# W2's Hadamard transform in pieces within attention's steps, the running sum ahead of the transposes, and tile-wise reuse of memory

## The chip, the cores and the metric

The kernel runs on one core of one Trainium2 chip. The metric is the device time of one execution in microseconds; three runs of the kernel before gave a median of 3984.01 us (3983.97 to 3985.0). Engines are named TensorE (PE in the profile), VectorE (DVE), ScalarE (ACT), GpSimd (POOL) and SyncE (SP), whose queue issues every transfer of this kernel.

## The reference, cut to what matters

One transformer layer with post-norms on x of 2 x 2048 x 512, all in f32:

```python
q, k, v, s = heads(x @ Wq), heads(x @ Wk), heads(x @ Wv), clip(heads(x @ Ws), -32, 32)
z = cumlogsumexp(s, axis=time)            # 16 heads, 64 keys, 64 slots, 128 values
p, g = exp(s - z), exp(shift(z) - z)
hk = scan(hk * g + k p);  pv = softmax(q hk)   # over the 64 slots
hv = scan(hv * g + p v);  o = pv hv
o = rmsnorm(o) * g_norm_weight * silu(x @ Wg)
x = layernorm(x + o @ Wo)
hidden = silu(x @ W1.T) * (x @ W3.T)      # 2048 wide
hidden = fwht(hidden)                     # Walsh-Hadamard transform, scaled by 1/sqrt(2048)
x = layernorm(x + hidden @ W2.T)
```

The transform is linear and symmetric, so it can be applied to W2 (512 x 2048) once instead of to `hidden` for every token. The kernel does that, before and after the change.

## The kernel before, in words

**Products.** Every large matrix product is a 2 x 2 block product made with 7 block multiplications instead of 8 (Strassen's scheme). `LEFT` and `RIGHT` (L89, L90) say which sums of blocks enter product k, `SUM` (L91) into which of the three PSUM sums c1, c2, c3 it is accumulated. For that, weights and activations are kept as 7 blocks: three as they are, and four sums and differences.

**W2's transform (L104 to L152).** In front of everything else. For each of four 128-row tiles of W2, it loads four pieces of 128 x 512 (L120), transposes each on TensorE (L125), multiplies them by a 128 x 128 Hadamard matrix (L130), which does 7 of the 11 butterfly stages, and does the other 4 on VectorE (L139, L140), each as an addition and a subtraction of 1024 columns. Then the 7 blocks are formed for each of 8 column blocks (L146 to L151), and stored to `w2s` in DRAM in one transfer of 896 KB each (L152).

**Attention (L161 to L654).** 4 groups of 4 heads, and in each 16 steps of 128 time positions for both batches: 64 steps. `run` (L551) writes a step's work by hand, in one order for TensorE, VectorE, ScalarE and GpSimd (`manual_schedule`): the products of this step (`now`), the second half of attention of the step before (`before`), the output projection that ends the one before that (`old`), and the input of the next (`new`). SP's queue is not in that order: a scheduler places the transfers. In the parts that the change touches:

- q1 to q7 are the products with `wqks` (L320), v1 to v7 those with `wvg` (L350), o1 to o7 those with `wo` (L533). `into` (L267) copies products 1, 5 and 6 on ScalarE (L273) and adds the others to them on VectorE (L278). o's results are added to `rows` (L529), which `store_rows` writes to `yd` (L546). Each engine works through its queue in order.
- `ps` is one PSUM tile of four banks, used in turn by `make_x` (L302), r's transposes (L452), the scores (L397, L400, L459, L464), `slots` (L412, L419), `values` (L476, L482), k's and E's transposes (L371, L373), the running sum (L378) and o's transposes (L517).
- `values` ends with a square on ScalarE (L487), a product on VectorE (L489), the addition to hv (L494) and a sum (L496). The next use of `ps` by TensorE is `k_e_transposed` (L367), copied out by L375; after one product of v, `running_sum` (L377) multiplies `e2` by a triangular matrix, z is copied (L380), and its reciprocal is taken in two halves (L389). The `scores` (L397) follow after another product of v, and their masking (L405), which `slots` (L412) needs.
- The first `Weights` are loaded ahead of the steps, `wqks`, `wvg` and `wo` in this order, and their four sums each (`sums`, L211) are made there, before any step. In later groups loads and sums lie within the steps. All weights share one buffer for the fourth block (`low`).

**FFN (L657 to L840).** Two halves of 16 tiles of 128 tokens. `load_tokens` reads `yd` (L676), transposes and forms 7 blocks, `load_weights` does so for W1 and W3 in the first half, `up` makes the two products and the gate, `down` the product with W2's blocks from `w2s` (L786, L799). Its pools are opened when attention's are closed. A pool's first tiles then wait until all of what lay in that memory is done.

The lines are those of the profile:

Of the kernel before, what the change touches and what calls it, by code (L numbers as in the profile page):

```python
# [14 lines left out]
P = 128  # L15
# [18 lines left out]
def gated_slot_attention_ffn_kernel(  # L34
# [69 lines left out]
    with ExitStack() as prep:  # L104
        rawp = prep.enter_context(tc.tile_pool(name="rawp", bufs=4))
        hp = prep.enter_context(tc.tile_pool(name="hp", bufs=2))
        wp = prep.enter_context(tc.tile_pool(name="w2p", bufs=1))
        ptp = prep.enter_context(tc.tile_pool(name="ptp2", bufs=4, space=PSUM))
        ppj = prep.enter_context(tc.tile_pool(name="ppj2", bufs=4, space=PSUM))
        hm = rawp.tile([P, P], F32, name="hm", bufs=1)  # L110
        nc.sync.dma_start(out=hm, in_=had)
        w2h = wp.tile([P, NFB, D], F32, name="w2h")

        for dt in range(KC):
            t0 = hp.tile([P, NFB, P], F32, name="t0")
            for q in range(NFB // 4):
                raw = rawp.tile([P, 4 * P], F32, name="raw")
                nc.sync.dma_start(  # L120
                    out=raw, in_=w2[dt * P : (dt + 1) * P, q * 4 * P : (q + 1) * 4 * P]
                )
                tp = ptp.tile([P, 4, P], F32, name="tp")
                for c in range(4):
                    nc.tensor.transpose(tp[:, c, :], raw[:, c * P : (c + 1) * P], ident)  # L125
                nc.scalar.copy(t0[:, 4 * q : 4 * q + 4, :], tp)
            t1 = hp.tile([P, NFB, P], F32, name="t1")
            for q in range(NFB // 4):
                pj = ppj.tile([P, 4, P], F32, name="pj")
                nc.tensor.matmul(pj, lhsT=hm, rhs=t0[:, 4 * q : 4 * q + 4, :], start=True, stop=True)  # L130
                nc.scalar.copy(t1[:, 4 * q : 4 * q + 4, :], pj)
            src, dst = t1, t0
            s = 1
            while s < NFB:
                if 2 * s == NFB:
                    dst = w2h[:, :, dt * P : (dt + 1) * P]
                a = src.rearrange("p (a two s) d -> p a two s d", two=2, s=s)
                o = dst.rearrange("p (a two s) d -> p a two s d", two=2, s=s)
                nc.vector.tensor_tensor(o[:, :, 0], a[:, :, 0], a[:, :, 1], ALU.add)  # L139
                nc.vector.tensor_tensor(o[:, :, 1], a[:, :, 0], a[:, :, 1], ALU.subtract)  # L140
                src, dst = dst, src
                s *= 2
        for hb in range(NPB):
            b = [w2h[:, hb + i * NPB, j * HD : (j + 1) * HD] for i in range(2) for j in range(2)]
            wt = hp.tile([P, 7, HD], F32, name="wt")
            nc.scalar.copy(wt[:, 0, :], b[0])  # L146
            nc.scalar.copy(wt[:, 1:3, :], w2h[:, hb + NPB, :].rearrange("p (j d) -> p j d", j=2))
            nc.vector.tensor_tensor(wt[:, 3, :], b[1], b[0], ALU.subtract)
            nc.gpsimd.tensor_tensor(wt[:, 5, :], b[3], b[1], ALU.subtract)
            nc.vector.tensor_tensor(wt[:, 4, :], b[3], wt[:, 3, :], ALU.subtract)  # L150
            nc.vector.tensor_tensor(wt[:, 6, :], b[2], wt[:, 4, :], ALU.subtract)  # L151
            nc.sync.dma_start(out=w2s[hb], in_=wt)  # L152

# [7 lines left out]
    with ExitStack() as att:  # L161
        wp = att.enter_context(tc.tile_pool(name="wp", bufs=1))
        xp = att.enter_context(tc.tile_pool(name="xp", bufs=2))
        yp = att.enter_context(tc.tile_pool(name="yp", bufs=6))
        keep = att.enter_context(tc.tile_pool(name="keep", bufs=1))
        c2 = att.enter_context(tc.tile_pool(name="c2", bufs=2))
        c1 = att.enter_context(tc.tile_pool(name="c1", bufs=1))
        pps = att.enter_context(tc.tile_pool(name="pps", bufs=1, space=PSUM))
# [5 lines left out]
        def bank(at, width=P):  # L174
            return ps[:, at].rearrange("p (i t) -> p i t", t=width)
# [371 lines left out]

        steps = [Step(g, n) for g in range(NG) for n in range(NCB)]
        w, nw = {}, {}

        def run(new, now, before, old):  # L551
# [10 lines left out]
            opens = now is not None and now.first  # L562

# [4 lines left out]
            do(new, "load_x")  # L568
# [4 lines left out]
            if opens and g:  # L573
                nw["vg"].sums(0)
# [5 lines left out]
            if opens and g:  # L580
                nw["vg"].sums(1)
            do(now, "q", 6)
            if opens and g:
                nw["vg"].sums(2)
            do(now, "q", 3)
            do(old, "store_rows")
# [3 lines left out]
            if opens and g:  # L590
                nw["vg"].sums(3)
# [10 lines left out]
            if o_last:  # L602
                nw["o"].sums(0)
            do(now, "k_e_transposed")
            do(now, "v", 2)
            if o_last:
                nw["o"].sums(1)
            do(now, "running_sum")
# [6 lines left out]
            if o_last:  # L615
                nw["o"].sums(2)
# [12 lines left out]
            if o_last:  # L629
                nw["o"].sums(3)  # L630
# [11 lines left out]
        with tc.manual_schedule(  # L642
# [3 lines left out]
            for name, load in (("qks", load_qks), ("vg", load_vg), ("o", load_o)):  # L646
                nw[name] = load(0)
            steps[0].make_x()
            for name in ("qks", "vg", "o"):
                for k in range(4):  # L650
                    nw[name].sums(k)
# [229 lines left out]
```

## Time and profile before

| | us |
|---|---|
| median of three runs | 3984.01 |
| the profiled execution | 3988.88 |
| its span | 3987.0 |
| TensorE busy | 3794.3 (95%) |
| VectorE busy | 1997.0 (50%) |
| ScalarE busy | 974.7 (24%) |
| GpSimd busy | 794.6 (20%) |
| one step of attention, first group | 41.67 |
| one step, later groups | 40.79 |

The span is the time between the first and the last event that the profiler saw of this execution. Busy times overlap. TensorE's clock is granted by a throttle; the page gives it in tenths of full speed, and it is full in all but a few slices. A row of the order of time gives the start, the length, the engine, the line, the operation, what it writes and reads, the number of instructions merged in the row, and in brackets how long the engine had been idle and what ended that. The length of a step was read from the distance between L489 in one step and in the next.

### The profile page before, as it was taken

Reading aid. Unit: us, or ns where it says so; the run is one execution under the profiler, and the core shown is the slowest. Engines: PE = TensorE matmul, PEld = TensorE weight load, DVE = VectorE, ACT = ScalarE, POOL = GpSimd, SP = SyncE. Lnnn points to the kernel's source line nnn. Section 1 sums busy time; section 2 is a strip of 40 time slices with the busy share of each in tenths; the row PEclk is TensorE's granted clock in tenths of the full one; section 3 lists DMA queues with packets and bytes.
Section 4 is the critical chain, followed back from the end, with each engine's and each line's share of the span. In section 5 each row is a group of like instructions: output and inputs, shape, how many; then the busy total and the mean of one; then the engine's idle time right before and its main releaser. Section 6 shows DMA issues by size and latency. Waiting matters only on the chain.

```text
span 3987.0 us, 57889 instructions
## 1 busy us (share of the span) xinstructions
PE 3794.3 (95%) x24416; PEld 2660.0 (67%) x24416; DVE 1997.0 (50%) x3012; ACT 974.7 (24%) x1637; POOL 794.6 (20%) x797
## 2 busy tenths in 40 slices
PE   3999999999999999999999999997999999999999
PEld 2777777777777777777767777774466466466466
DVE  6555555655455565545565565654434334334334
ACT  2222222222222222222222222222211211211210
POOL 1122222112121221212112222222311211211211
PEclk6999999999999999999999999998999999999999
DMA  5212121211111121111121111113322212322220
GB/s 182 72 52 76 51 74 54 88 60 46 55 41 60 52 86 51 50 51 41 60 76 60 59 55 56 42 45 122 129 95 99 112 74 95 114 77 85 110 82 21
DMA packets 110371, 290.19 MB, mean 73 GB/s; under 512 B 12704, under 2 KB 37408, under 8 KB 106016
## 3 DMA queue, kind: packets, MB, share of 16 engines
q1 hardware_dynamic: 110112, 286.50, 20.9%
q8 instruction: 192, 3.15, 0.3%
q14 instruction: 67, 0.55, 0.0%
HBM read 207.68 MB, written 78.64 MB: 72 GB/s over the span
## 4 chain that ended last, share of the span: by engine, by line
PE 88%; DVE 7%; ACT 2%; DMA 2%; issue 1%; POOL 1%; SPq 0%; POOLq 0%; DVEq 0%; ACTq 0%
PE c L731 19%; PE c L350 16%; PE c L320 15%; PE c L533 9%; PE c L799 9%; PE ps L476 3%; DVE t L489 2%; PE ps L459 2%; PE ps L397 2%; ACT sq L487 2%; PE ps L412 2%; PE ps L482 1%; PE ps L517 1%; PE ps L464 1%; PE ps L378 1%; PE ps L400 1%
## 5 line engine op out<-in xcount | busy, mean ns | idle before, releaser
L350 PE MATMUL c<-wvg,xb 128*128 128x512 f32 x1792 | 864.8, 605 | 0.0
L731 PE MATMUL c<-xb,w 128*128 128x512 f32 x1792 | 777.6, 594 | 0.7 <-ACT w L707 0.7
L731 PEld LDWEIGHTS c<-xb,w 128*128 128x128 f32 x1792 | 339.5, 190 | 414.4 <-issue 403.6
L320 PE MATMUL c<-xb,wqks 128*128 128x128 f32 x3584 | 556.7, 278 | 4.2 <-DVE rows L529 2.0
L320 PEld LDWEIGHTS c<-xb,wqks 128*128 128x128 f32 x3584 | 492.6, 193 | 26.9 <-DVE rows L529 3.2
L350 PEld LDWEIGHTS c<-wvg,xb 128*128 128x128 f32 x1792 | 311.0, 190 | 267.3 <-issue 258.0
L799 PE MATMUL c<-w2t,hid 128*128 128x256 f32 x1792 | 400.8, 383 | 17.0 <-DVE res L806 17.0
L278 DVE TENSOR_TENSOR t<-c,kept 128x384 f32<-128x384 f32 (+1 forms) x384 | 235.0, 612 | 335.4 <-PE c L320 222.7
L799 PEld LDWEIGHTS c<-w2t,hid 128*128 128x128 f32 x1792 | 340.8, 192 | 74.2 <-DVE res L806 26.7
L273 ACT COPY kept<-c 128x384 f32<-128x384 f32 (+1 forms) x384 | 203.4, 530 | 674.3 <-PE c L320 548.3
L320 PE MATMUL c<-wqks,xb 128*128 128x128 f32 x1792 | 348.3, 276 | 1.0 <-DMA wqks<-in_L_attn_Ws 1.0
L743 DVE TENSOR_TENSOR out<-c,kept 128x512 f32<-128x512 f32 x192 | 131.7, 686 | 336.4 <-PE c L731 336.3
L529 DVE TENSOR_TENSOR rows<-c,rows 128x256 f32<-128x256 f32 x448 | 182.6, 418 | 192.5 <-PE c L533 190.8
L320 PEld LDWEIGHTS c<-wqks,xb 128*128 128x128 f32 x1792 | 273.7, 193 | 1.3 <-DMA wqks<-in_L_attn_Ws 1.3
L738 ACT COPY kept<-c 128x512 f32<-128x512 f32 x192 | 112.6, 586 | 614.9 <-PE c L731 614.9
L389 DVE RECIPROCAL iz<-z 128x256 f32<-128x256 f32 x128 | 223.6, 1747 | 47.8 <-ACT z L380 47.8
L337 POOL TENSOR_TENSOR e<-e,zc 1x512 f32<-1x512 f32 x60 | 75.9, 1264 | 801.0 <-ACT e L336 801.0
L489 DVE TENSOR_TENSOR t<-ps,t 128x1024 f32<-128x1024 f32 x64 | 78.4, 1225 | 290.6 <-ACT sq L487 290.6
L806 DVE TENSOR_TENSOR res<-c,res 128x256 f32<-128x256 f32 x224 | 94.7, 423 | 253.0 <-PE c L799 252.9
L443 POOL TENSOR_TENSOR r<-r,iz 128x512 f32<-128x512 f32 x64 | 81.4, 1272 | 642.8 <-DVE sm L441 642.8
L767 POOL TENSOR_TENSOR hid<-hid,a 128x512 f32<-128x512 f32 x32 | 40.7, 1272 | 704.5 <-DVE a L750 704.5
L437 ACT ACTIVATE r<-r 128x512 f32<-128x512 f32 x64 | 40.3, 630 | 459.9 <-DVE r L436 459.9
(166 smaller groups left out, 4792.2 us busy)
## 6 DMA issues: line engine op xcount, KB each, us to landing
xb<-xd SPq DMA_DIRECT2D x48, 896.0 KB, 4.6
w<-w13s SPq DMA_DIRECT2D x24, 1792.0 KB, 7.4
yd<-rows SPq DMA_DIRECT2D x128, 256.0 KB, 2.2
w2t<-w2s SPq DMA_DIRECT2D x32, 896.0 KB, 7.0
rows<-yd SPq DMA_DIRECT2D x96, 256.0 KB, 2.7
xd<-xb SPq DMA_DIRECT2D x16, 896.0 KB, 3.6
w13s<-w SPq DMA_DIRECT2D x8, 1792.0 KB, 6.0
raw<-in_L_ffn_W SPq DMA_DIRECT2D x48, 256.0 KB, 3.1
```

The lines of the kernel that those rows point to most:

```text
L273: nc.scalar.copy(self.kept[k], s)
L278: nc.vector.tensor_tensor(t[:, to], s, self.kept[other], ALU.add)
L320: nc.tensor.matmul(out[:, i * P : (i + 1) * P], lhsT=a, rhs=b, start=(k in OPENS and c == 0 and i == 0), stop=(c == 1), skip_group_check=True,
L350: nc.tensor.matmul(out, lhsT=self.xb[:, RIGHT[k], c, :], rhs=w["vg"].t[:, LEFT[k], c, :], start=(k in OPENS and c == 0), stop=(c == 1), sk ...
L389: nc.vector.reciprocal(self.iz[:, h], self.z[:, h])
L476: nc.tensor.matmul(po[th, j, i], lhsT=self.a2[:, j, i, th], rhs=self.value(i, j), start=self.first, stop=True, skip_group_check=True,)
L489: nc.vector.tensor_tensor(self.gj, po, self.gj, ALU.mult)
L529: nc.vector.tensor_tensor(y_, self.uo.sum(k), y_, ALU.add)
L533: nc.tensor.matmul(out, lhsT=self.ob[:, RIGHT[k], c, :], rhs=w["o"].t[:, LEFT[k], c, :], start=(k in OPENS and c == 0), stop=(c == 1), ski ...
L731: nc.tensor.matmul(s[i][SUM[k]], lhsT=w[:, i, LEFT[k], c, :], rhs=xb[:, RIGHT[k], c, :], start=(k in (1, 2, 5) and c == 0), stop=(c == 1), ...
L743: nc.vector.tensor_tensor(t, s[i][c], kept[i][k], ALU.add)
L799: nc.tensor.matmul(s[SUM[m]], lhsT=hids[p][:, LEFT[m], k * P : (k + 1) * P], rhs=w[p][:, RIGHT[m], :], start=(m in (1, 2, 5) and p == 0), ...
```

## The change

- The transform's block in front is gone. A generator `hadamard` does the same work for two pairs of W2's row tiles, (0, 2) and (1, 3), in pieces; `run` takes the next piece at three places of each step whose `new` step belongs to group 1 or later: after `make_x`, after `row_stats` and after q3. A piece is the issue of one raw load; or four transposes and their copy; or one product with the Hadamard matrix and its copy; or one of the four stages for one tile; or the differences and the last store for one column block. Stages come once a step. Transposes and products use banks 0 and 1 of `ps`. The blocks are written to `w2s` in four transfers for each column block and pair, three of 64 KB straight from the transformed tiles and one of 256 KB with the four differences. The raw tiles take a buffer of the pool for rows, which gets 7 buffers instead of 6.
- `running_sum` is called before v2 and `k_e_transposed` after it, the other way round than before.
- Ahead of the steps, step 1's x is loaded right after `wqks`, and only `wqks`'s sums are made there. `wvg`'s and `wo`'s first sums are made within step 0, as in later groups.
- The FFN's pools are opened with `reuse_waits="tile"`: a tile's first use then waits only for the tiles that lay in its memory.

```diff
-    with ExitStack() as prep:
...
-        for dt in range(KC):
-            t0 = hp.tile([P, NFB, P], F32, name="t0")
...
-            nc.sync.dma_start(out=w2s[hb], in_=wt)
...
-        yp = att.enter_context(tc.tile_pool(name="yp", bufs=6))
+        yp = att.enter_context(tc.tile_pool(name="yp", bufs=7))
...
+        hp = att.enter_context(tc.tile_pool(name="hp", bufs=1))
...
+        def hadamard():
+            for pair in ((0, 2), (1, 3)):
+                wh = [hp.tile([P, NFB, P], F32, name=f"wh{i}") for i in range(2)]
+                ping = hp.tile([P, NFB, P], F32, name="ping")
+                def stage(i, s):
+                    src, dst = (wh[i], ping) if s % 2 == 0 else (ping, wh[i])
+                    a = src.rearrange("p (a two s) d -> p a two s d", two=2, s=1 << s)
+                    o = dst.rearrange("p (a two s) d -> p a two s d", two=2, s=1 << s)
+                    nc.vector.tensor_tensor(o[:, :, 0], a[:, :, 0], a[:, :, 1], ALU.add)
+                    nc.vector.tensor_tensor(o[:, :, 1], a[:, :, 0], a[:, :, 1], ALU.subtract)
+                for i, dt in enumerate(pair):
+                    for q in range(NFB // 4):
+                        raw = yp.tile([P, D], F32, name="raw", tag="rows")
+                        nc.sync.dma_start(out=raw, in_=w2[dt * P : (dt + 1) * P, q * D : (q + 1) * D])
+                        yield
+                        for c in range(4):
+                            nc.tensor.transpose(bank(0)[:, c, :], raw[:, c * P : (c + 1) * P], ident)
+                        t0 = hp.tile([P, 4, P], F32, name="t0")
+                        nc.scalar.copy(t0, bank(0))
+                        yield
+                        nc.tensor.matmul(bank(1), lhsT=hm, rhs=t0, start=True, stop=True)
+                        nc.scalar.copy(wh[i][:, 4 * q : 4 * q + 4, :], bank(1))
+                        yield
+                for i in range(2):
+                    for s in range(4):
+                        stage(i, s)
+                        for _ in range(3):
+                            yield
+                j = pair[0] * P
+                for hb in range(NPB):
+                    b11, b21, b12, b22 = (wh[i][:, hb + h * NPB] for i in range(2) for h in range(2))
+                    wt = hp.tile([P, 4, P], F32, name="wt")
+                    nc.vector.tensor_tensor(wt[:, 0], b12, b11, ALU.subtract)
+                    nc.gpsimd.tensor_tensor(wt[:, 2], b22, b12, ALU.subtract)
+                    nc.vector.tensor_tensor(wt[:, 1], b22, wt[:, 0], ALU.subtract)
+                    nc.gpsimd.tensor_tensor(wt[:, 3], b21, wt[:, 1], ALU.subtract)
+                    o = w2s[hb][:, :, j : j + P]
+                    for at, b in enumerate((b11, b21, b22)):
+                        nc.sync.dma_start(out=o[:, at], in_=b)
+                    nc.sync.dma_start(out=o[:, 3:7], in_=wt)
+                    yield
+                    if hb % 2:
+                        yield
...
+            if prepare:
+                next(w2_work, None)
-            if opens and g:
+            if opens:
                 nw["vg"].sums(0)
...
+            do(now, "running_sum")
+            do(now, "v", 2)
...
             do(now, "k_e_transposed")
-            do(now, "v", 2)
...
-            do(now, "running_sum")
...
-            for name, load in (("qks", load_qks), ("vg", load_vg), ("o", load_o)):
-                nw[name] = load(0)
+            nw["qks"] = load_qks(0)
+            steps[1].load_x()
+            nw["vg"] = load_vg(0)
+            nw["o"] = load_o(0)
             steps[0].make_x()
...
-    xp = ctx.enter_context(tc.tile_pool(name="fxb", bufs=1))
+    xp = ctx.enter_context(tc.tile_pool(name="fxb", bufs=1, reuse_waits="tile"))
...
```

The last line stands for all nine pools of the FFN.

## The prediction

> **What bounds the kernel now.** I read the busy shares first, then the windows by stage, then the waits of TensorE, then the order of time in the places that the change touches. TensorE is busy 95% of the span, so a stage gains only where TensorE stands still. The windows (busy time per engine, number of instructions, granted clock, DMA share, GB/s) show where:
>
> ```profile
> 0.00:78.00 78.00, 27.80 (x96) 15.60 (x96) 50.46 (x56) 26.16 (x49) 9.69 (x21) 0.72 0.44 156
> 78.00:112.00 34.00, 18.99 (x99) 17.18 (x100) 15.27 (x19) 3.16 (x7) 6.04 (x6) 0.58 0.85 267
> 771.00:2712.00 1941.00, 1881.24 (x15080) 1415.71 (x15080) 1088.04 (x1574) 525.45 (x859) 406.29 (x393) 1.00 0.17 54
> 2712.00:2767.00 55.00, 30.52 (x168) 22.81 (x166) 19.70 (x36) 9.25 (x19) 12.50 (x17) 0.77 0.34 115
> ```
>
> There are two holes: the first 112 us (W2's transform, then the first loads of attention) and 2712 to 2767 (attention's tail and the start of the FFN). Between them TensorE is busy 97%. The largest wait left in attention's steps, by the list of waits (us in total, times, longest), is
>
> ```profile
> PE ps L371 <- DVE hv L494: 59.5, 56, 1.1
> ```
>
> In order of time, the first hole and one ordinary step read (start, length, engine, what, idle before it):
>
> ```profile
> 74.03 2.62 SPq L293 DMA_DIRECT2D xin<-in_L_attn_hidden_states  x3
> ...
> 94.66 1.23 DVE L217 TENSOR_TENSOR wvg<-low,wvg 128x1024 f32<-128x1024 f32 x1 [4.57 <-DMA low<-in_L_attn_Wg]
> 98.19 2.45 DVE L223 TENSOR_TENSOR wvg<-wvg 128x1024 f32<-128x1024 f32 x1
> 101.70 1.11 PE L302 MATMUL ps<-ident,xin 128*128 128x128 f32 x4 [10.50 <-DMA xin<-in_L_attn_hidden_states]
> 112.20 3.60 PE L350 MATMUL c<-wvg,xb 128*128 128x512 f32 x8
> ...
> 1264.03 0.66 PE L371 MATMUL ps<-ident,t 128*128 128x128 f32 x4 [1.06 <-DVE hv L494]
> 1266.67 1.02 PE L378 MATMUL ps<-e,causal 128*128 128x512 f32 x2
> 1267.53 1.88 PE L350 MATMUL c<-wvg,xb 128*128 128x512 f32 x4
> 1267.73 0.59 ACT L380 COPY z<-ps 128x512 f32<-128x512 f32 x1 [1.56 <-PE ps L378]
> ```
>
> Attention's first load is issued only at 74.03; TensorE then waits 10.50 us for step 1's x, queued behind all weights, and reaches the first v product at 112.20.
>
> **1. W2's transform leaves the front, and the loads there change order.** If the front only moved up, the first xin would be issued at about 1.6 (where the first raw load stood) instead of 74.03: 72.4 us. The new order gives more. SP issues every 0.47 us: gn, hm, two xin, so the first Wq goes out at about 2.6. Before, 16.1 us passed from the first Wq (78.58) to the first sum of wvg (94.66). Now three low tiles and step 1's x (0.9 MB, 3.4 us at the 267 GB/s of the window) lie in front too, while SP's 2.6 us stop for the shared low tile falls beside transfers in flight: 19.5 to 22.1, I take 20.8. wvg's sums are now written between q's additions on VectorE, so q2's, q3's and q7's additions stand behind that landing, and TensorE's q4 behind q7's: three sums at a pitch of 1.15 and three additions at 0.5 make 5.0 us, so q4 starts at 25.9 after some 5 us of idleness.
>
> Here the skill's clock rule (TensorE: Matmul & The Clock Gate, Part 1: The HAM clock gate) speaks against the change: an idle window of about 3.4 us halves the clock, and as long a busy one restores it. The row: after the 10.5 us wait the granted clock was 0.50 from 101 to 106 and 1.00 from 107. By the rule 3.4 us at half speed cost 1.7 us, by the row 5 us cost 2.4. I take the row: q4 needs 2.1 instead of 1.3, the first v product starts at about 28.0, and as if at full clock at 29.4. **Gain 112.2 - 29.4 = 83 us** (72 to 86).
>
> wo's sums move from the front into step 0. VectorE is busy 15.7 of the 34.7 us there, and the first product with wo comes at the end of step 1: nothing; without that cover 2.8 us.
>
> **2. The pieces in the steps.** Three places a step from step 15 on: A after o7, B before q6, C after q3.
>
> *TensorE.* 16 times four transposes (B) and one 128x512 product of two passes (C). Four equal transposes (L452) hold TensorE 0.44 us, and L378, the same product, 0.86 (1266.67 to 1267.53). In these places TensorE has no wait to fill, so both count. And a wait is added: in the built program the transposes of r (L452) wait for the copy of C's product out of the memory that they share, although it is another bank. The row for that is L378 and L380: the copy ends at 1268.32, TensorE would have gone on at 1267.53, so 0.84 with the wake-up. Behind it stand q7 and scores2, that is the whole engine. 0.44 + 0.86 + 0.84 and a bare weight load make 2.2 us; **16 x 2.2 = 35 us lost** (21 if the wait is covered, 42 if B waits alike). B's transposes write bank 0 and q6 follows with no new wait; C finds its copy (0.59 on ScalarE) done during q6 and q3 (2.7 us).
>
> *The raw loads.* 16 DMAs of 256 KB (3.1 us to landing). SP isn't ordered by hand: the built order issues each at least a step (40.8 us) before its transposes. Nothing; if issued at A, 2.2 us before B, see the rival.
>
> *VectorE.* 16 stages of two 1024-column operations (1.22 each, as L139): 2.4 us at A. They start after o7's addition (about 1287.6 in the step above), so q2's addition comes at 1290.1 instead of 1288.6, o4's at 1290.7; q3's, due one step after 1251.37 at 1292.2, is on time. q4 waits only for q7's. Nothing on TensorE; uncovered it would be 16 x 2.4 = 39 us.
>
> *The differences.* 16 times two 128-column subtractions on VectorE and two on GpSimd, then one 256 KB store, with one buffer. At B the next one stands in VectorE's queue until A's store has landed (about 1 us of arithmetic, 0.4 issue, 3 landing: 1292), with q3's addition behind it, late by 0.5 us, and q7's, due at 1293.9, on time. The skill (SBUF — State Buffer, SBUF: two separate sides) speaks against the arrangement: VectorE with two SBUF inputs and GpSimd exclude each other for a whole instruction. The trace agrees: L223 took 2.45 us instead of 1.22 while GpSimd scaled wo. By the row for 256 columns (0.72 on GpSimd) I estimate 0.5 for each of 32, so 1 us more per piece on VectorE: by the rule 16 us on that engine, by the step's row of idleness before q3's addition (2.32) none on TensorE. In step 32, where wvg's sums share the places, I put 1 us. **1 us lost** (0 to 16).
>
> *SP.* 48 stores of 64 KB and 16 of 256 KB replace 8 of 896 KB; at 0.4 us each the largest cluster (16, in one step) holds SP 6.5 us. Behind it wait the loads of xb and rows, issued most of a step before use (xb at 1279.34 for a step that begins at 1322). Nothing.
>
> **3. The running sum ahead of the transposes.** It seems made for the 59.5 us above, since its bank is free after L489, 0.6 us before L494. But the built program makes it wait for L494 as well: the moved wait is the same, 1.06. The transposes then wait for z's copy, which ends 1.65 us after the running sum starts; the v product between ends after 2.58. The first reciprocal starts 2.6 us earlier on an idle VectorE, but L405, the next that TensorE needs, waits for the scores either way. **0** (34 gained if the wait were L489's, -5 if a copy is uncovered).
>
> **4. Tile-wise reuse.** Order and buffers of the FFN stay; only first uses wait for less. The chain of waits there:
>
> ```profile
> 2747.87 3.25 DMA yt<-yd
> 2751.12 0.04 issue
> 2751.16 0.65 PE tp L679 x4
> 2751.82 6.22 DMA yt<-yd
> 2758.03 0.14 issue
> 2758.17 2.89 PE tp L679 x12
> 2761.06 0.02 issue
> 2761.08 4.31 DMA raw<-in_L_ffn_W
> ```
>
> The first three yt now wait for the last v product (about 2712) and stand behind step 62's stores, so they land long before 2747. The fourth is still behind the last stores of rows (2751.7), and these behind the last layer norm. But w2t's 896 KB, which ran ahead of it, are gone by then: 3 us instead of 6.2. **Gain 4 us** (2 to 8).
>
> **Sum** against the profiled execution: span 3987.0 - 83 + 35 + 1 - 4 = 3936. That execution took 3988.88, and the median of the runs (3984.01) is 3.0 below the span; so 3984 - 51 = **3933 us**, 1.3% faster.
>
> **Rivals.**
> - *The pieces cost TensorE less* (the copy's wait is covered, or the FFN's start gains 8): 3984 - 83 + 21 - 8 = 3914. For it: ScalarE is busy 24%. Against: TensorE has nothing else in order.
> - *VectorE's pieces reach TensorE.* Up to 39 + 16: 3988 at the far end, some 20 more likely, 3953. For it: VectorE runs in order, and the pieces stand ahead of additions that TensorE waits for. Against: the idle times above.
> - *The swap does what it looks like*: 34 more, 3899. Against: the built wait.
> - *The raw tiles land late, and the kernel gets slower.* Place: B. If SP held each raw load until A, behind two stores of rows (2.2 us to landing) and its own 3.1, TensorE would wait about 3 us, and beyond that half the clock goes for 5 us (2.4 lost): 16 x 5.4 = 86, so 4019. It decides from 51/16 = 3.2 us per piece. Against: the built order.
> - *The front doesn't follow its loads* and only moves up: 11 less, 3944, inside my range.
>
> **How the numbers follow.** Forecast 0.62 (3922 to 3945), cheap pieces 0.13, VectorE 0.16, swap 0.03, late raw tiles 0.04, no change 0.02 (gains and losses cancel). Below 3914 and above 3955 I leave about 0.08 each. 0.2% (8 us) is about what a measurement of this kernel can tell. Faster 0.93, within it 0.03, slower 0.04.
>
> **What would show it.** In the new profile: the first v product near 28 us and the clock at 0.5 just before; a wait of TensorE at r's transposes on ScalarE's copy of the transform, 16 times 0.8; the wait for L494 now at the running sum, 56 times 1.06; yt's first wait gone, the second near 3 us; steps with stages as long as before (40.79), those with products 2.2 longer. It is wrong if stage steps grow, if B's transposes wait for raw tiles, or if wvg's landing comes past 25 us.

## The result, and the profile after

The changed kernel took 3943.61 us (median of 4 runs, 3941.05 to 3946.23), the kernel before on the same chip 3983.99 (3982.28 to 3985.0). The ratio is 0.9899, 95% interval 0.9882 to 0.9916: 1.0% faster, 40 us. The forecast was 3933 with 3914 to 3955 around it. The size is 10.6 us short of the forecast, and the terms of the sum are not all the ones that I wrote down.

The profiled execution took 3946.23 us, its span is 3944.4 (before 3987.0). First the windows of the changed kernel, the first and the last cut at the same events as those shown of before, the middle one equally long (busy time per engine with the number of instructions, for PE, PEld, DVE, ACT and POOL; granted clock; DMA share; GB/s):

```profile
0.00:27.20 27.20, 16.45 (x100) 15.03 (x101) 11.52 (x15) 4.44 (x8) 8.23 (x19) 1.00 0.84 269
729.00:2670.00 1941.00, 1866.66 (x14922) 1397.16 (x14923) 1105.92 (x1609) 531.39 (x869) 417.12 (x420) 1.00 0.18 58
2670.00:2725.50 55.50, 29.94 (x165) 23.15 (x163) 18.82 (x35) 8.65 (x18) 11.05 (x16) 0.74 0.35 117
```

The first hole has shrunk from 112 us to 27. The second, attention's tail and the FFN's start, is 55 us as before. In between, TensorE is busy 1866.66 of 1941 us where it was busy 1881.24: the steps now have more idleness than before, not less. The list of TensorE's waits in the changed kernel (us in total, times, longest) names it:

```profile
PE ps L329 <- DVE hv L445: 64.6, 56, 1.2
PE c L817 <- DVE res L824: 16.9, 16, 2.4
PE tp L697 <- DMA yt<-yd: 12.2, 4, 5.4
PE ps L403 <- ACT wh L530: 10.9, 16, 0.7
```

The wait for the addition to hv has moved from the transposes to the running sum (L329), and grown from 59.5 to 64.6 us. The wait of r's transposes (L403) for the copy of W2's product is new, 16 times 0.68. The first hole and one ordinary step of the changed kernel in order of time (start, length, engine, what, idle before it and what ended it):

```profile
20.82 1.23 DVE L168 TENSOR_TENSOR wvg<-low,wvg 128x1024 f32<-128x1024 f32 x1 [1.38 <-DMA low<-in_L_attn_Wg]
25.81 0.68 PE L271 MATMUL c<-xb,wqks 128*128 128x128 f32 x4 [2.70 <-issue]
27.23 3.60 PE L301 MATMUL c<-wvg,xb 128*128 128x512 f32 x8
...
1237.36 1.98 PE L301 MATMUL c<-wvg,xb 128*128 128x512 f32 x4
1240.49 1.10 PE L329 MATMUL ps<-e,causal 128*128 128x512 f32 x2 [1.15 <-DVE hv L445]
1241.43 1.88 PE L301 MATMUL c<-wvg,xb 128*128 128x512 f32 x4
1243.15 0.60 PE L322 MATMUL ps<-ident,t 128*128 128x128 f32 x4
1243.58 0.60 PE L324 MATMUL ps<-ident,e 128*128 128x128 f32 x4
1244.02 1.88 PE L301 MATMUL c<-wvg,xb 128*128 128x512 f32 x4
```

The first v product starts at 27.23 (before 112.20). From one v product to the next but one (L301, 1237.36 to 1244.02) 6.66 us pass; in the step shown of before, the same stretch was 1260.98 to 1267.53, 6.55.

The gate product of each step (L489 before, L440 after, VectorE) is a good milestone, because it follows the last scores of every step. From one to the next is the step's length. With it the span splits like this (us; the second profile is another profiled execution of the same kernel):

| stretch | before | after | difference | second profile |
| --- | --- | --- | --- | --- |
| start to the first gate product | 146.72 | 61.74 | -85.0 | 62.06 |
| first to last gate product, 63 steps | 2581.54 | 2625.11 | +43.6 | 2623.50 |
| last gate product to the FFN's first product | 39.08 | 38.61 | -0.5 | 38.56 |
| FFN's first product to the end | 1219.7 | 1219.0 | -0.7 | 1217.9 |
| span | 3987.0 | 3944.4 | -42.6 | 3942.0 |

And the steps by kind: ordinary steps 40.79 before, 40.90 after (41.67 and 41.78 in the first group of heads); steps in which a stage of W2's transform runs on VectorE 40.90 too; steps with transposes and a product of W2's transform 43.10. So 63 times 0.11 is 6.9 us, 16 times 2.20 is 35.2, together 42.1. The pieces on TensorE cost what the forecast said, the swap cost some 7 us where it said nothing, and the FFN's start gave almost nothing where it said 4.

### The profile page after: what moved, and what is told of

The parts are those of the page before. It is cut to its first block, busy times and chain, and to the rows that moved or that the text cites. A ratio compares the mean times of both kernels' runs of the same rounds, so it can differ in the third digit from the quotient of the medians.

```text
span 3944.4 us, 57882 instructions
## 1 busy us (share of the span) xinstructions
PE 3786.3 (96%) x24416; PEld 2649.9 (67%) x24416; DVE 1981.4 (50%) x3020; ACT 967.4 (25%) x1621; POOL 803.8 (20%) x821
## 4 chain that ended last, share of the span: by engine, by line
PE 88%; DVE 6%; ACT 2%; issue 1%; DMA 1%; POOL 1%; SPq 0%; POOLq 0%; DVEq 0%; ACTq 0%
PE c L749 19%; PE c L301 16%; PE c L271 15%; PE c L484 9%; PE c L817 9%; PE ps L427 3%; DVE t L440 2%; PE ps L410 2%; PE ps L329 2%; ACT sq L438 2%; PE ps L363 2%; PE ps L348 2%; PE ps L468 1%; PE ps L433 1%; PE ps L415 1%
## 5 line engine op out<-in xcount | busy, mean ns | idle before, releaser
L301 PE MATMUL c<-wvg,xb 128*128 128x512 f32 x1792 | 863.5, 604 | 0.0
L749 PE MATMUL c<-xb,w 128*128 128x512 f32 x1792 | 777.7, 594 | 0.7 <-ACT w L725 0.7
L749 PEld LDWEIGHTS c<-xb,w 128*128 128x128 f32 x1792 | 339.6, 190 | 414.3 <-issue 404.6
L301 PEld LDWEIGHTS c<-wvg,xb 128*128 128x128 f32 x1792 | 310.4, 190 | 266.1 <-issue 256.9
L817 PE MATMUL c<-w2t,hid 128*128 128x256 f32 x1792 | 399.2, 382 | 16.9 <-DVE res L824 16.9
L440 DVE TENSOR_TENSOR t<-ps,t 128x1024 f32<-128x1024 f32 x64 | 78.4, 1224 | 292.2 <-ACT sq L438 292.2
L824 DVE TENSOR_TENSOR res<-c,res 128x256 f32<-128x256 f32 x224 | 94.6, 423 | 252.8 <-PE c L817 252.8
L356 DVE TENSOR_TENSOR a<-ps,causal 128x1024 f32<-128x1024 f32 x64 | 78.3, 1224 | 198.2 <-issue 188.5
```

The lines of the kernel that those rows point to most:

```text
L301: nc.tensor.matmul(out, lhsT=self.xb[:, RIGHT[k], c, :], rhs=w["vg"].t[:, LEFT[k], c, :], start=(k in OPENS and c == 0), stop=(c == 1), sk ...
L440: nc.vector.tensor_tensor(self.gj, po, self.gj, ALU.mult)
L749: nc.tensor.matmul(s[i][SUM[k]], lhsT=w[:, i, LEFT[k], c, :], rhs=xb[:, RIGHT[k], c, :], start=(k in (1, 2, 5) and c == 0), stop=(c == 1), ...
L817: nc.tensor.matmul(s[SUM[m]], lhsT=hids[p][:, LEFT[m], k * P : (k + 1) * P], rhs=w[p][:, RIGHT[m], :], start=(m in (1, 2, 5) and p == 0), ...
```

## The experiments

All times below stand beside the same kernel before (3984.6 to 3987.4 us in these sets of runs), to which the ratios refer. The changed kernel itself was repeated once, beside the kernels of sections 3 and 4, and came at 3944.35; where another section's kernel is set against it, the 3 us between the kernels before of the two sets stay uncertain. Since the front and the FFN also differ by some us from one execution to the next, the steps' lengths are the sharper measure: but for the few at a change of the group of heads, they repeat to 0.01 us.

### 1. The swap, and why the wait stayed

The theory: the running sum needs banks 0 and 1 only, whose last reader is the gate product; it waits for hv's addition because waits are kept by whole tiles, and all four banks are one tile. Four kernels take that apart. The first undoes the swap alone:

```
-            do(now, "running_sum")
+            do(now, "k_e_transposed")
             do(now, "v", 2)
             ...
-            do(now, "k_e_transposed")
+            do(now, "running_sum")
```

> The changed kernel with the swap alone undone: k's and E's transposes first, the running sum after the second v product. Theory (the swap costs, because the running sum's two weight loads now stand behind the wait for the addition to hv, where a transpose with one load stood): every step 0.11 us shorter, 60 steps, so 7 us less than the changed kernel's 3943.6, about 3937, and the running sum no longer named in the list of waits. Rival (the 0.11 us per step come from something else, VectorE's pieces or the seventh rows buffer): no change, 3944.

Measured: 3934.63 us (3932.82 to 3939.33), ratio 0.9872 (0.9855 to 0.9888). The steps are 40.79 and 41.67 again, 63 steps 5.9 us shorter than in the second profile of the changed kernel (forecast 7). Of the 10.9 us between these two spans the other 5.0 lie in the front (0.3), the FFN's start (1.4) and the FFN (3.3), where this edit has nothing to act on. The list of waits has the old line back, 59.5 us at the transposes. So the swap by itself costs 0.11 us a step. The rows show where: the transposes started 0.06 us after hv's end (1263.97 to 1264.03) and held TensorE 0.49 (0.43 is what four take in a stream); the running sum starts 0.14 after it (1240.35 to 1240.49) and holds it 0.94 (0.86 in a stream). The forecast put this down to the running sum's weight loads; that they are the reason was not tried apart.

The second keeps the swap and splits the tile; no bank moves, and no operation is added or reordered:

```
-        ps = pps.tile([P, 4, 512], F32, name="ps")
+        ps = [pps.tile([P, 2, 512], F32, name=f"ps{i}") for i in range(2)]
 ...
-            return ps[:, at].rearrange("p (i t) -> p i t", t=width)
+            return ps[at // 2][:, at % 2].rearrange("p (i t) -> p i t", t=width)
```

> The changed kernel with the PSUM tile of four banks declared as two tiles of two banks; every bank stays where it is and no operation is added or moved. Theory (the wait for the addition to hv is there because waits are kept by whole tiles: banks 0 and 1, which the running sum needs, are free after the gate product): the Square starts when the values are done and not the hv products behind them (0.8 us earlier), the running sum waits for the gate product only, and the 1.15 us of idleness plus the 0.1 of restart go from about 58 steps: 66 to 73 us less, 3871 to 3878. If only the running sum's wait moves and the Square does not: 0.6 x 58 = 35 less, 3909. Rival (the wait only changes its name, the transposes then wait as long for hv): 3940 to 3944.

Measured: 3860.23 us (3857.29 to 3861.48), ratio 0.9680 (0.9666 to 0.9694): 84 us less than the changed kernel. Steps of 39.51 and 40.39, 1.39 shorter than the changed kernel's, where I had forecast 1.25 (1.15 of idleness and 0.1 of restart; 66 to 73 us in all). A step of this kernel in order of time, TensorE first, then ScalarE, then VectorE:

```profile
1198.91 1.97 PE L427 MATMUL ps<-t,a 128*64 128x128 f32 x32
1200.71 1.04 PE L433 MATMUL ps<-t,e 128*64 128x128 f32 x16
1201.68 1.98 PE L301 MATMUL c<-wvg,xb 128*128 128x512 f32 x4
1203.50 1.02 PE L329 MATMUL ps<-e,causal 128*128 128x512 f32 x2
1204.36 1.88 PE L301 MATMUL c<-wvg,xb 128*128 128x512 f32 x4
...
1200.92 1.02 ACT L438 ACTIVATE sq<-ps 128x1024 f32<-128x1024 f32 x1 [0.83 <-PE ps L427]
...
1201.98 1.23 DVE L440 TENSOR_TENSOR t<-ps,t 128x1024 f32<-128x1024 f32 x1 [3.74 <-ACT sq L438]
1203.12 0.68 DVE L445 TENSOR_TENSOR hv<-hv,ps 128x512 f32<-128x512 f32 x1
```

Two waits went. The running sum (L329) starts at 1203.50 with no idleness ahead of it, while hv's addition still runs until 1203.80. It follows 1.82 us after the start of the v product ahead of it (1201.68), though that product's row is 1.98 long. The list of waits counts idleness from the end of such a row, and so leaves out 0.16: a wait listed at 1.15 cost 1.15 + 0.16 + 0.08 of slower running behind it, and these are the 1.39. And the Square (L438) starts on the values (L427), not on hv's products behind them (L433): the changed kernel, in the step shown above, had

```profile
1237.47 1.02 ACT L438 ACTIVATE sq<-ps 128x1024 f32<-128x1024 f32 x1 [1.70 <-PE ps L433]
1238.53 1.23 DVE L440 TENSOR_TENSOR t<-ps,t 128x1024 f32<-128x1024 f32 x1 [4.62 <-ACT sq L438]
1239.67 0.68 DVE L445 TENSOR_TENSOR hv<-hv,ps 128x512 f32<-128x512 f32 x1
```

From the start of the values to the Square it is 2.88 us there (1234.59 to 1237.47) and 2.01 with two tiles. That second wait I had not seen when I forecast the change: I had followed the wait of TensorE to hv, and not asked what hv's addition had itself waited for.

The third has the two tiles and the old order:

> Two tiles of two banks as in the run before, and the swap undone: the transposes stand first and wait for the addition to hv, which comes 0.6 us after the gate product. Theory: hv is about 0.8 us earlier than in the changed kernel, so of the 1.15 us of idleness 0.2 to 0.4 stay, in 56 steps: 11 to 22 us more than with two tiles and the swap, 3885 to 3897. This is what the swap is worth once the tiles allow it. Rival (the swap is worth nothing in either arrangement): the same time as with two tiles and the swap.

Measured: 3880.07 us (3876.59 to 3883.34), ratio 0.9731 (0.9716 to 0.9745). Steps of 39.92 and 40.80, and in the list of waits

```profile
PE ps L322 <- DVE hv L445: 10.6, 56, 0.2
```

So on two tiles the swap is worth 0.41 us in an ordinary step and 20 us in all (forecast 11 to 22), and on one it costs 0.11 a step. The last of this group is the kernel before with two tiles and nothing else:

> The kernel before with its PSUM tile of four banks declared as two tiles of two, nothing else. In the changed kernel with the swap undone, which has the order of before, two tiles brought 0.87 us in each of 63 steps, 54.5 us in all. If the gain belongs to the two tiles and not to the change: 3984 - 54.5 = 3930, steps of 39.9 (41.67 to 40.8 in the first group), and the whole change on two tiles is then worth 3930 - 3860 = 70 us where it was worth 40 on one tile.

Measured: 3924.71 us (3923.93 to 3925.38), ratio 0.9844 (0.9828 to 0.9860). Its steps are 39.92 and 40.80 as well, and 63 of them take 2525.95 us, 55.6 less than before. The tile's split alone is worth more than the whole change. On two tiles the change is worth about 3924.7 - 3860.2 = 64 us, where it was worth 40 on one.

### 2. The place of W2's product

```
             do(now, "q", 6)
 ...
+            if prepare:
+                next(w2_work, None)
             do(now, "q", 3)
-            if prepare:
-                next(w2_work, None)
             do(old, "store_rows")
```

> The changed kernel with the third place of the steps (where W2's transform product stands) moved from after q3 to before q3; the second place (transposes) stays before q6. Theory (r's transposes wait for the copy of the transform's product only because they follow it at once): q3's 1.3 us hide the copy, the 0.68 us of wait go from 16 steps, 11 us less, 3932.5; and the product now has q6's 1.3 us between the transposes and itself, enough for the 0.6 us copy of t0. Rival (the product then waits for t0's copy as long as r's transposes did): no change, 3944.

Measured: 3927.74 us (3927.56 to 3927.98), ratio 0.9850 (0.9836 to 0.9865), 16 us less than the changed kernel, where 11 were forecast. The steps with a product are 42.20 long instead of 43.10, the others in mid-group unchanged; 16 times 0.90 is 14.4. TensorE in order of time in the changed kernel, around the product (L529) and r's transposes (L403):

```profile
896.31 1.02 PE L529 MATMUL ps<-t,hm 128*128 128x512 f32 x2
898.01 0.66 PE L403 MATMUL ps<-ident,r 128*128 128x128 f32 x4 [0.68 <-ACT wh L530]
898.50 0.61 PE L271 MATMUL c<-xb,wqks 128*128 128x128 f32 x4
```

The same place with the product before q3:

```profile
849.13 1.02 PE L529 MATMUL ps<-t,hm 128*128 128x512 f32 x2
849.99 0.61 PE L271 MATMUL c<-xb,wqks 128*128 128x128 f32 x4
...
851.33 0.60 PE L403 MATMUL ps<-ident,r 128*128 128x128 f32 x4
851.77 0.61 PE L271 MATMUL c<-xb,wqks 128*128 128x128 f32 x4
```

With q3 between them (849.99 to 851.33) r's transposes have nothing to wait for. What is left of the piece is 42.20 - 40.90 = 1.30: exactly 0.44 for four transposes and 0.86 for the product. The 0.90 that went were the listed wait of 0.68, the 0.16 by which the product's row (1.02) is longer than the 0.86 after which the next instruction follows it in a stream, and 0.06 in r's transposes, which held TensorE 0.49 behind the wait (898.01 to 898.50) and 0.44 without it. The forecast had counted the 0.68 alone.

### 3. The front's order

```
             nw["qks"] = load_qks(0)
-            steps[1].load_x()
             nw["vg"] = load_vg(0)
             nw["o"] = load_o(0)
+            steps[1].load_x()
             steps[0].make_x()
-            for k in range(4):
-                nw["qks"].sums(k)
+            for name in ("qks", "vg", "o"):
+                for k in range(4):
+                    nw[name].sums(k)
```

(and the sums of wvg and wo inside step 0 left out, since they are done here.)

> The changed kernel with the loads and sums of attention's front in the order of before: step 1's x behind all weights, all twelve sums ahead of step 0. W2's pieces stay in the steps. Theory (83 us of the front are 72 of moving up and 11 of the new order): the first v product comes at 112.2 - 72.4 = 39.8 instead of 27.2, so 12 to 13 us more than the changed kernel, 3956. Rival (the new order brings nothing, everything came from leaving W2's transform out of the front): no change, 3944.

Measured: 3950.91 us (3948.88 to 3956.27), ratio 0.9916 (0.9901 to 0.9930), against 3944.35 for the changed kernel in the same set. The first v product came at 33.52, 6.0 us after the 27.54 of the changed kernel's second profile, and not 12.6. Neither theory had it right. TensorE waited 6.04 us for step 1's x, not 10.50 as before. The x was issued at 15.43, ahead of Wo's last low tile (23.09); in the kernel before, one of its two tiles was issued behind that tile (97.47, behind 97.05). SP's order is not written by hand, so this kernel is no full return to the old order, and the split of the 85 us is only half answered: 6.0 for the order, 79 for the rest, of which 72.4 are the moving up. The other 6.3 (from 112.20 to 33.52 it is 78.7) can be read from the rows of the two kernels: from the first load to the start of the wait for step 1's x it is 14.5 us and was 17.2, the wait is 4.5 shorter, and from its end to the first v product it is 11.4 and was 10.5.

### 4. The FFN's start

> The changed kernel itself once more, beside the three next runs on the same chip, for a second look at the start of the FFN. If the 38.6 us that passed in the first profile from the last gate product of attention to the first product of the FFN were a property of the kernel, they come again (38.2 to 39.0); if the landing of the last tokens varies from execution to execution (e1 to e3, which have the same FFN, showed 35.0 to 37.9), another value within 35 to 39. Time 3940 to 3948.

(e1 to e3 are the kernels of sections 1 and 2.) Measured: 3944.35 us, and 38.56 us from the last gate product to the FFN's first product. So 38.6 came again, though the four kernels of sections 1 and 2 on the changed kernel's FFN had 34.9 to 37.8. But it came by another path. In the second profile TensorE's waits behind the first of its waits for tokens were 3.61 us instead of 5.76 (1.86 and 1.75 for 2.47 and 3.29), and it stood 2.50 us for the first piece of W1 instead, which in the first profile had landed by then:

```profile
2722.31 1.08 PE L723 MATMUL tp<-ident,raw 128*128 128x128 f32 x4 [2.50 <-DMA raw<-in_L_ffn_W]
```

What is late there depends on what the transfers meet, and two equal times are no proof of one cause.

The reuse by tiles, undone on all FFN pools:

```
-    rawp = ctx.enter_context(tc.tile_pool(name="fraw", bufs=3, reuse_waits="tile"))
+    rawp = ctx.enter_context(tc.tile_pool(name="fraw", bufs=3))
 ...
```

> The changed kernel with its FFN pools reusing memory as a whole again, as before. Theory (tile-wise reuse lets the first three token tiles load ahead of the last step, and later transfers give part of it back): from attention's last gate product to the FFN's first product 39.1 us as before, against 35.0 to 38.6 with tile-wise reuse, so 0.5 to 4 us more, 3944 to 3948. Rival (the reuse brings nothing): no change.

Measured: 3945.16 us (3942.94 to 3945.64), ratio 0.9898 (0.9883 to 0.9913), against 0.9901 for the changed kernel: no difference. The stretch took 37.76 us, inside the 34.9 to 38.6 of the kernels with reuse by tiles. The first three token loads are now issued at 2704.15 instead of 2681.70, and it makes nothing later: the FFN's first product waits for the last tokens, whose rows are stored at the very end in either case.

The last kernel of this group keeps the reuse and holds back the first four W2 tiles:

```
             t = w2p.tile([P, 7, HD], F32, name="w2t")
+            if blk == 0 and first == 0:
+                nc.gpsimd.tensor_copy(t[:, 0, 0:1], hids[0][:, 6, 0:1])
             nc.sync.dma_start(out=t, in_=w2s[p])
```

> The changed kernel with the first four W2 tiles of the FFN (896 KB each, first needed some 200 us later) made to wait for the first hidden block, by a copy of one column of it into each tile on GpSimd ahead of its load, which the load overwrites. Theory (two of these transfers are issued between the token loads and delay them: the last two tokens landed 7.7 us after issue instead of 2.8): the last token tiles land about 3 us after issue, and the first FFN product comes 35 us or less after attention's last gate product, 3.5 us sooner than the 38.6 of the first profile. Rival (the tokens are late for another reason): 37 to 39 us as before.

Measured: 3941.98 us (3938.52 to 3943.28), ratio 0.9890 (0.9875 to 0.9905). The total doesn't separate from the changed kernel's, the stretch does: 33.68 us from the last gate product to the first FFN product, 4.9 less than in the second profile (33.34 in the kernel of section 6, which has the same edit). TensorE's token transposes (L697) and the first product (L749) in order of time, in the changed kernel's first profile:

```profile
2713.01 1.94 PE L697 MATMUL tp<-ident,yt 128*128 128x128 f32 x8 [5.41 <-DMA yt<-yd]
2717.41 1.09 PE L697 MATMUL tp<-ident,yt 128*128 128x128 f32 x4 [2.47 <-DMA yt<-yd]
2721.78 1.94 PE L697 MATMUL tp<-ident,yt 128*128 128x128 f32 x8 [3.29 <-DMA yt<-yd]
2725.46 5.41 PE L749 MATMUL c<-xb,w 128*128 128x512 f32 x6 [0.73 <-ACT w L725]
```

and with W2's first tiles late:

```profile
2711.43 2.88 PE L697 MATMUL tp<-ident,yt 128*128 128x128 f32 x12 [5.63 <-DMA yt<-yd]
2715.41 0.63 PE L697 MATMUL tp<-ident,yt 128*128 128x128 f32 x4 [1.10 <-DMA yt<-yd]
2716.62 0.63 PE L697 MATMUL tp<-ident,yt 128*128 128x128 f32 x4 [0.58 <-DMA yt<-yd]
2719.04 1.13 PE L749 MATMUL c<-xb,w 128*128 128x512 f32 x2 [0.73 <-ACT w L725]
```

The waits behind the first shrink from 5.76 us (2.47 and 3.29; 3.61 in the second profile) to 1.68. In the changed kernel SP issued in this order (start, length, what, how many):

```profile
2710.17 1.34 SPq L694 DMA_DIRECT2D yt<-yd  x3
2711.60 0.38 SPq L804 DMA_DIRECT2D w2t<-w2s  x1
2714.12 1.22 SPq L694 DMA_DIRECT2D yt<-yd  x2
```

896 KB of W2 stood between the sixth and the seventh token tile of 256 KB, and TensorE began on the last two 7.7 us after the first of them was issued (2714.12 to 2721.78; 5.5 in the second profile). With W2's tiles out of the way it is about 3 us (2713.40 to 2716.62 for the last). So the theory holds for the tokens: the transfers of tiles that are needed only four hidden blocks later took time that the early tokens had won. Not all of the 4.9 stays: TensorE now stands 1.47 us for VectorE (L728) a little later, and the end of the FFN's sixth matmul comes 3.8 us sooner than in the second profile.

### 5. What VectorE had left

```
                         stage(i, s)
+                        stage(i, s)
```

> The changed kernel with every one of the 16 stages of W2's transform on VectorE done twice (the second time with the same result), so 2.4 us more VectorE work at the first place of 16 steps. Theory (these stages lie in VectorE's idle time between o7's addition and q7's, of which TensorE needs only q7's, two microseconds later): steps with a stage stay at 40.9 us, 3944. Rival (the stages fill the gap to the brim): 16 x 2.4 = 39 us more, 3983.

Measured: 3946.53 us (one run). The steps with a stage in mid-group are 40.90 long: 2.4 us more work in the place that the forecast called covered cost nothing. The 63 steps together took 3.5 us more than in the second profile. Of these 2.8 lie in steps 47 and 49, which have a stage at a change of the group of heads, where the weights' sums share VectorE (43.62 and 45.88 for 42.00 and 44.73). The other 0.7 lie in step 31 (43.29 for 42.55), which has no stage.

> The same with every stage done four times, 7.3 us more VectorE work in each of 16 steps. Theory (a reserve of some 3.5 us: in a step of the changed kernel q7's addition would end at 1316.9 where TensorE starts q4 at 1313.1, so q4 comes 3.7 us late): steps with a stage 40.9 + 3.7 = 44.6, in all 16 x 3.7 = 59 more, 4003. Rival (VectorE, 55 to 75% busy in such a step, takes it in): 40.9 and 3944. Upper end, nothing hidden: 16 x 7.3 = 117.

Measured: 4012.82 us (one run). The 63 steps took 72.3 us more than in the second profile. The 13 stage steps in mid-group are 43.7 to 46.7 long, 44.7 on average where 44.6 was forecast: 3.8 more each. The three at a change of the group (47 to 49) took 22.0 more together, and that is what carries the total past the 4003 of the forecast. The list of waits has a new entry,

```profile
PE c L271 <- DVE t L229: 51.9, 17, 6.1
```

which is q4 waiting for q7's addition, as the theory named it. By its rows the added work is 6.8 us a step (six operations 1.135 apart), and 3.8 of it show, so the reserve of a stage step in mid-group is about 3 us, a little less than the 3.5 that I had read from one step. At a change of the group the three steps lost more (22.0) than the work added to them (20.4).

### 6. The three edits together

Two tiles, the product before q3, the first W2 tiles late:

> The changed kernel with the three edits that made it faster alone: two PSUM tiles instead of one (3860.2), W2's transform product before q3 (3927.7), the FFN's first W2 tiles late (3942.0). If they add up: 3944 - 84 - 16 - 2 = 3842. If the product before q3 gains less because with two tiles other waits come behind r's transposes, or the FFN's start is bound by the W1 and W3 tiles then: up to 3850.

Measured: 3844.42 us (3841.52 to 3845.76), ratio 0.9642 (0.9627 to 0.9656). They add up. The 63 steps take 2527.97 us, 95.5 less than in the second profile of the changed kernel, and the two edits of the steps alone had given 81.4 and 14.2. This is 3.6% faster than the kernel before, and 100 us faster than the changed kernel.

## Why the forecast was right, and where it was not

**The front: -83, measured -85.0; right, one part not.** wvg's first sum was forecast at 20.8 and began at 20.82, TensorE's q4 at 25.9 and began at 25.81. The idleness before q4 was not 5 us but 2.70: TensorE was at work until 23.1, and not until 20.9 as I had it. The half clock that I charged for it (2.4 us by the row of before, an estimated 1.7 by the Trainium skill's rule in TensorE: Matmul & The Clock Gate, Part 1: The HAM clock gate, of about 3.4 us idle) did not come: four q products took 0.68 and 0.61 us behind the wait, as at full clock. In the kernel with the front's order undone a wait of 6.04 us stood in the same place, and its windows show it (same columns as above):

```profile
22.00:26.00 4.00, 3.88 (x19) 3.91 (x20) 3.96 (x3) 0.86 (x2) 2.40 (x1) 0.50 0.69 255
26.00:30.00 4.00, 4.00 (x36) 4.00 (x36) 3.37 (x6) 0.48 (x1) 1.27 (x1) 0.96 1.02 333
```

2.70 us of idleness with no loss and 6.04 with about 4 us at half clock fit the rule's 3.4 on both sides. The rule was applicable; the idleness that I put into it was wrong. A sharp limit it is not, since once 1.91 us were enough (last section).

**The pieces on TensorE: +35, measured 16 x 2.20 = 35.2; right.** The parts are 0.44 + 0.86 as taken from the rows of before (1.30 by the run with the product before q3), the 0.84 of wait as forecast (0.68 by the list, but 0.84 from 897.17, where TensorE would have gone on, to 898.01), and 0.06 of slower transposes where I had put a weight load. That r's transposes would wait for the copy, out of another bank of the same tile, was forecast from the built order, and came 16 times.

**VectorE's pieces: 0 and +1; right.** Stage steps are as long as ordinary ones. With the work doubled they still are, and beyond about 3 us of extra work they are not. The rival in which these pieces reach TensorE is answered by that: even twice the work doesn't reach it in mid-group. The differences cost their 1 us where the forecast had put it, in the step that it calls 32 (the 31st of the 63), in which wvg's sums share the places. VectorE stood 1.78 us until the first piece's store had landed, and q4 then waited for q7's addition:

```profile
1352.62 0.29 DVE L541 TENSOR_TENSOR wt<-wh,wh 128x128 f32<-128x128 f32 x1 [1.78 <-DMA w2s<-wt]
1356.89 0.71 PE L271 MATMUL c<-xb,wqks 128*128 128x128 f32 x4 [0.81 <-DVE t L229]
```

In the second profile the wait is 0.48. The kernel before has none there, and the changed kernel has none at the change of the group that falls on stages, nor in the other steps with differences. The Trainium skill's rule in SBUF — State Buffer (SBUF: two separate sides), that VectorE with two SBUF inputs and GpSimd exclude each other, shows in kind where the two overlap: in five of the 16 pieces the second subtraction took 0.43 or 0.47 us beside GpSimd's instead of 0.29. That is at most some 0.18 per piece where I had estimated 1 us. The raw tiles, the rival on the slower side, appear in no wait of TensorE.

**The swap: 0, measured +6.9 by the steps' lengths (+5.9 by the run that undoes it); the step that failed first.** "The moved wait is the same, 1.06" was nearly so (1.15), but I carried the wait over and not what stands behind it: how soon the new instruction starts once released, and how much of it runs at the pace of a stream. The bound that I gave on the losing side, 5 us, was for another mechanism and too small. And I had named the reason for all of it, that the built program makes the sum wait for L494 though its bank is free after L489, without asking what causes that. The rival "the swap does what it looks like" lay there at 0.03: rightly for this kernel, but another declaration of one tile turns it on.

**Tile-wise reuse: -4, measured -0.5, and nothing by the run that undoes it; the step that failed second.** The first three token tiles did land early, their 2.8 us of wait are gone, and TensorE began on the fourth 2.8 us after its issue (2710.17 to 2713.01), as forecast. The failing step is "w2t's 896 KB, which ran ahead of it, are gone by then". One of these tiles was gone; the next stood between the sixth and the seventh token. I cleared the way for one transfer of the queue and did not ask who else would start sooner because of it.

**What is left.** In the first profile the last step's values (L427) took 3.31 us behind the same idleness of 1.91 us after which they took 1.97 in the second: 1.3 us of one execution. The median of the changed kernel lies 0.8 below that span, not 3.0 as I had carried over from before. From 3933, with -2.0 for the front, +7.6 for the 63 steps (the swap and this 1.3; the steps at a change of the group differ by some tenths), +3.5 for the FFN's start, -0.7 for the FFN and +2.2 for the median, one is at 3943.6. The time lay within the range because the misses were small against it: 13.3 us one way and 2.7 the other, so they hardly cancelled.

## What to carry to other kernels

When the built program makes an instruction wait for something that its data do not need, look for the object in which both are kept before pricing the wait as given: here one PSUM tile over four banks cost the kernel before 55 us in 63 steps, by a wait of ScalarE that the list of TensorE's waits does not name, and turned a reordering worth 20 us into a loss of 6 or 7. A wait is moved with its restart; follow it back link by link, because the thing waited for may wait needlessly itself. And where a load is made to start earlier, list all transfers that its queue releases with it, and see whether those that are needed last can be held back.

## What the runs showed of the hardware that I had not expected

- A wait of TensorE costs more than the idleness listed for it. Ahead of it 0.16 us are hidden in the row of the instruction before (1.98 for a pace of 1.82, 1.02 for 0.86), and behind it the first instruction runs slower (transposes by 0.06 us, the running sum by 0.08). Taking the waits out gained 0.90 us where 0.68 were listed and 1.39 where 1.15 were.
- What is released counts too: behind the same addition, the transposes started 0.06 us after its end and the running sum 0.14.
- The clock after the same idleness is not always the same. In the changed kernel's first profile TensorE stood 1.91 us before the last step's values, and took 3.31 over them, at a granted clock of 0.50 from 2683 to 2686:

```profile
2682.44 3.31 PE L427 MATMUL ps<-t,a 128*64 128x128 f32 x32 [1.91 <-DVE a L420]
```

In its second profile, as in the twelve other kernels profiled, the same instructions behind the same wait took 1.97:

```profile
2682.49 1.97 PE L427 MATMUL ps<-t,a 128*64 128x128 f32 x32 [1.91 <-DVE a L420]
```

- The column of the granted clock is blind at a program's start. It says 1.00 for the first 27 us of the changed kernel, but four q products took 1.06 us until about 16 and 0.61 from 17 on; and in the kernel before four of them took 1.06 where the column said 0.50 (102.60) and 0.61 where it said 1.00 (107.25). So the durations tell the clock there, not the column.
- The time from the FFN's first product to the end varied from 1214.5 to 1219.0 us among the changed kernel's two profiles and those of the kernels of sections 1 and 2 that share its FFN. In the two of 1214.5 TensorE's wait for the addition to `res` (L824) is 14.4 and 14.9 us in all, in the four others 16.9 to 17.1; what the rest is was not tried.
